# Rows for the last product in the spectrum's buffer, and a new table of times

## The chip, the cores and the metric

One core of a Trainium2 chip runs the whole program. The metric is the device time of one execution in microseconds (us). The engines are PE (TensorE: matmuls, with PEld for its weight loads), DVE (VectorE), ACT (ScalarE) and POOL (GpSimd); SP (SyncE) issues the transfers of the steady state. Each engine works through its own queue in order and waits there for what the next instruction needs.

## The reference

Input are 64 images of 96 x 56 x 56 in fp32. Each goes through two blocks:

```python
# block 0: convolution
out = silu(bn(expand_w @ x))                      # 1x1, 96 -> 192
out = channel_shuffle(shift_groups(out), 4)
out = silu(bn(bn(depthwise3x3(out)) + bn(id_w * out)))
se  = sigmoid(grouped1x1(relu(grouped1x1(mean(out)))))
x   = silu(bn(proj_w @ (out * se)) + x)           # 192 -> 96
# block 1: tokens t = 56*56 x 96
h = relu(bn(layernorm(t) @ w1.T))                 # 96 -> 192
X = fft(h, axis=tokens, norm='ortho')
X = relu(X.real*rd - X.imag*id + rb) + 1j*relu(X.imag*rd + X.real*id + ib)
t = t + bn(ifft(X).real @ w2.T)                   # 192 -> 96
t = t + ffn(layernorm(t))                         # 96 -> 384 -> 96, rounded to an 8-bit format
```

## The kernel before

The images go through some 60 kinds of step, each a small function `step(b, i)` for image `b` and part `i`. The transform over 3136 tokens is done in two stages of length 56: `f1` along one axis, `f2` along the other with the twiddles in its table, and `w2`, `i1`, `i2` back. Between the stages the data changes its layout by a trip through DRAM: `f1_st` writes the spectrum (`spec`), `f2_ld` reads it in four parts; `i1_st` writes `rows`, `i2_ld` reads them in two halves. A later part of each load is preceded by a tiny transfer into `probe` that reads what the earlier part brought, so SP waits there until that has landed.

The order of the work is written out by hand. `PLAN` gives each step and part a key, and the program is emitted in the order of `b * 105 + key`; every engine gets its instructions in that order. Keys of one image run from about -50 to over 370, so parts of up to four or five images are under way at a time. A key of 178.8 stands where the next image has 73.8. The numbers themselves set no time, only the order.

The steps, in the order in which an image meets them:

- `x_in` (SP) loads the image into `xi`, one buffer for all images. `ea_mm`/`ea_ev` and `eb_mm`/`eb_ev` (PE, ACT) expand, `eb_sh` (SP) shifts part of the channels from `e_u` into `e_b`, `eb_z` (POOL) clears its edge columns.
- `dw_mm`/`dw_ev` (PE, ACT), `gt`/`gs` and `lt`/`ls` (DVE, ACT) are three shares of the 3x3 convolution; `gt` and `lt` are nine passes of DVE each (L495, L508), `ls` is L511.
- `se1`, `se2` the gates; `se2_pw` (DVE) the gated weights; `pj_mm` (PE), `pj_add` (DVE, residual), `pj_ev` (ACT, L599) the projection into `t_buf`, of which there are three.
- `c_mm` (PE, L629), `c_st` (DVE, L637), `c_v`, `c_pow` (POOL, L656), `sp_v` (DVE, L661), `sp_mm` (PE), `sp_ev` (ACT), `sp_st` (SP) the statistics for the first norm.
- `w1_mm` (PE, L687) and `w1_ev` (DVE, L692) fill `h_v`; `f1_mm` (PE, L707), `f1_ev` (ACT, L719), `f1_st` (SP).
- `f2_ld` (SP) fills `g_v`; `f2_mm` (PE, L755 and L765), `f2_u` (ACT, L780), `f2_s` (DVE, L796 and L799), `f2_r` (ACT, L803), `f2_p` (DVE, L809) fill `pq_a` and `pq_b`.
- `w2_mm` (PE, L820 and L832), `w2_ev` (ACT, L850) fill `u_v`; `i1_mm` (PE, L859), `i1_ev` (ACT, L871) fill `q_v`; `i1_st` (SP).
- `i2_ld` (SP, L883 and L884) fills `p_v`; `i2_mm` (PE, L894), `i2_ev` (DVE, L906) add to `t_buf`.
- `n_mm` (PE, L607), `n_sq`, `n_v`, `n_pow` (POOL), `n_x`, `x_mm` (PE, L936), `x_ev` the second norm, turned by channels into `xq`; `h_mm` (PE, L949), `h_ev` (ACT, L954), `h_b` (DVE, L959), `h_q` (ACT, L965) and `o_mm` (PE, L971), `o_ev`, `o_b` (ACT, L981), `o_f` (POOL, L987), `o_st` (SP, L993) the last two products.

Two large buffers in SBUF serve several of these one after the other. `buf_h` holds `h_v`, then `pq_a` and `pq_b`, then `p_v`; `buf_g` holds `g_v`, then `u_v` (its first 2784 columns) and `q_v` (behind them). In PSUM, `psa` has two halves that `w1`, `f1`, `f2`, `w2`, `i1` and `i2` take in turn, and `psb` has four buffers for all other products.

PE's order of one period between the second product of the spectrum and the convolution, by the keys of before (a prime for each image further back): `f2_mm2'`, `se1_mm`, `f2_mm1'`, `h_mm7''`, `h_mm10''`, `se2_mm`, `o_mm1''`, `f2_mm3'`, `pj_mm0`, `pj_mm1`, `f2_mm4'`, `o_mm2''`, `w2_mm1'`, `h_mm9''`, `f2_mm5'`, `w2_mm0'`, `pj_mm2`, `pj_mm3`, `w2_mm2'`, `i1_mm0'`, two `h_mm''`, `i1_mm1'`, `h_mm18''`, `w2_mm3'`, two `h_mm''`, `c_mm2`, `c_mm0`, `i1_mm2'`, the other `c_mm`, four `eb_mm` of the next image, `sp_mm0`, three `ea_mm`, `i2_mm1'`, `i2_mm0'`, two `h_mm''`, `w1_mm0`, `sp_mm1`, `n_mm2'`, `n_mm0'`, `i2_mm3'`, `i2_mm2'`, `w1_mm1`, and so on to `f1_mm6`, `dw_mm`, `f2_mm0`, five small `h_mm` and `o_mm`.

Of the kernel before, what the change touches and what calls it, by code (L numbers as in the profile page):

```python
# [15 lines left out]
C = 96  # L16
# [19 lines left out]
NJ = HW // 2  # L36
# [7 lines left out]

PERIOD = 105.0000000
PLAN = {
    "x_in": (-47.0873800, -43.2480721, -33.8184146, -42.4321669, -41.6983245, -49.6354125, -45.2970245),
    "ea_mm": (25.6687554, -18.6019459, -18.2766274, 16.8947317, 9.0890490, -20.9491366, 26.5234594),
    "ea_ev": (26.5961203, -12.8346944, -12.0558905, 18.3539585, 11.9892739, -18.0927155, 26.8208273),
    "eb_mm": (-24.2217280, -27.1252465, -28.5212136, -26.0439145),  # L50
    "eb_ev": (-24.1705572, -24.8159248, -27.0548028, -24.4210050),
    "eb_sh": (-7.7763780, -5.1891020, -14.3493101, -8.0736385),
    "eb_z": (-0.0568513,),
    "dw_mm": (27.1905859, 28.2270849, 30.0157383),
    "dw_ev": (32.6265507, 32.5419044, 34.0136867, 32.0626837),
    "gt": (
        18.5417590, 27.3932657, 28.4348554, 30.0405776, 30.3534777, 31.2679969, 32.1252342, 33.5617949, 35.3971287,
    ),
    "gs": (37.3295953,),
    "lt": (-3.4369246, 1.4154043, 8.9015990, 12.7386339, 14.9242937, 16.9569681, 19.0058087, 25.8181102, 27.2536815),  # L60
    "ls": (30.9696760,),
    "se1_mm": (38.1174920,),
    "se1_ev": (39.4012005,),
    "se2_mm": (39.9568261,),
    "se2_ev": (41.0093676,),
    "se2_th": (41.6370568,),
    "se2_pw": (42.7356286,),
    "pj_mm": (47.6293895, 48.0460084, 55.6924205, 56.2257124),
    "pj_add": (51.9548047, 52.9757229, 48.9486048, 52.4199992, 56.5208084, 56.3342891, 57.7357223, 58.9053497),
    "pj_ev": (52.4266468, 54.5563910, 49.5686264, 53.9975302, 57.3353294, 58.0358601, 64.2278724, 60.1034130),  # L70
    "c_mm": (68.6422640, 72.8958869, 66.4186663, 70.5016788, 73.7968378, 81.1540053, 75.3642593),
    "c_st": (69.1048996, 74.0834508, 69.6641726, 71.8469708, 79.6401411, 81.2770733, 76.3014887),
    "c_v": (77.3368996, 84.7421070),
    "c_pow": (80.4785931, 85.6468413),
    "sp_v": (83.0231830, 86.9442643),
    "sp_mm": (83.5958606, 91.6622997),
    "sp_ev": (84.6935666, 98.3470105),
    "sp_st": (84.9182307, 104.3262665),
    "w1_mm": (91.1847046, 99.3743923, 107.0630638, 109.7535225, 115.0779331, 117.7791802, 128.3897698),
    "w1_ev": (95.1158413, 101.3844416, 109.5428488, 112.4130173, 118.6707781, 121.0948441, 130.1859056),  # L80
    "f1_mm": (103.1645366, 103.6378920, 112.1950558, 112.9967147, 121.9973686, 123.2339179, 131.7418102),
    "f1_ev": (103.8752244, 106.2876092, 115.0341529, 116.5416927, 123.1240239, 126.3577447, 132.9203119),
    "f1_st": (105.0265754, 116.1773780, 117.6886644, 118.9203869, 126.8918215, 126.9985321, 135.1083565),
    "f2_ld": (135.1419010, 135.4933209, 140.1563600, 153.2148099),
    "f2_mm": (135.3144599, 144.2623043, 142.7071223, 149.0540458, 153.9987769, 158.4518856),
    "f2_u": (
        137.6614180, 139.5999755, 145.8963285, 148.6480681, 143.6745056, 144.3798314, 151.9081888, 154.2916813,
        154.8766840, 155.4088772, 160.1561499, 160.2407000,
    ),
    "f2_s": (  # L90
        140.6001249, 141.6781807, 148.1048425, 149.2120807, 145.7714192, 145.9139389, 152.5732992, 154.5515294,
        156.3172941, 156.6391862, 160.5955754, 160.7678822,
    ),
    "f2_r": (143.2110272, 151.0363931, 149.4970293, 156.5551535, 160.8170295, 165.3808270),
    "f2_p": (145.3432078, 151.4176571, 149.5496523, 158.2621001, 161.1258051, 167.6494558),
    "w2_mm": (159.7753575, 155.3022495, 161.7965796, 168.1185810),
    "w2_ev": (161.2536676, 157.1569605, 163.6822311, 171.1138835),
    "i1_mm": (162.6590790, 166.7961018, 174.2991711),
    "i1_ev": (166.3472470, 165.9292538, 169.1177355, 169.1485805, 176.9253459, 176.6408078),
    "i1_st": (174.9466660, 180.3925690, 182.4974982),  # L100
    "i2_ld": (188.6796396, 198.8294222),
    "i2_mm": (192.8792346, 192.2221249, 201.7637940, 200.8210782),
    "i2_ev": (197.2438881, 196.4091824, 193.4196408, 195.1684356, 205.0085736, 204.5692890, 201.3823970, 201.8192486),
    "n_mm": (199.2735303, 219.3462979, 198.1616011, 209.7155720, 217.1048197, 206.4557874, 216.1525940),
    "n_sq": (200.3838494, 223.0303187, 198.7625009, 212.4039709, 219.3987946, 208.1995030, 218.5954397),
    "n_v": (200.8599777, 223.0993290, 200.2251649, 217.3989652, 220.1840919, 209.9338724, 219.1855594),
    "n_pow": (201.5854245, 224.4817921, 203.3394463, 218.3771210, 221.4663650, 210.8600116, 220.4581247),
    "n_x": (204.8989415, 227.0802149, 207.1755708, 219.2080326, 226.6324331, 212.4013872, 223.1334093),
    "x_mm": (205.9313777, 228.0541936, 214.7407205, 222.1417630, 227.6089704, 214.9482177, 224.9828165),
    "x_ev": (215.5949267, 230.5744237, 217.0784037, 224.8320339, 228.9853364, 216.6319969, 227.3901209),  # L110
    "h_mm": (
        232.6842970, 233.0509672, 234.5689910, 233.8905234, 243.9705701, 231.1824963, 242.0876641, 249.3422780,
        247.6714562, 262.3158746, 249.5121590, 269.1269742, 245.6772976, 281.8579222, 275.5176718, 291.0115353,
        298.8948961, 298.6901683, 272.9130353, 274.8890827, 267.7027131,
    ),
    "h_ev": (
        233.2951821, 233.9892274, 235.1790311, 235.3740739, 245.7427623, 232.8851785, 246.7755713, 250.3102318,
        248.5727503, 264.8834302, 250.8738180, 272.1122460, 247.3449184, 285.4922975, 280.0758001, 292.5182940,
        298.9075518, 299.1057623, 275.2554216, 280.8510059, 271.9477751,
    ),  # L120
    "h_b": (
        233.3310183, 238.5879932, 239.6985884, 236.4106010, 248.1860080, 237.7565907, 247.4859421, 252.4799898,
        253.3286109, 265.1753247, 274.5160827, 273.6196081, 259.8167793, 289.1079857, 281.7059923, 295.2166748,
        313.0427147, 307.8153028, 280.3205727, 295.0172563, 303.2860349,
    ),
    "h_q": (
        235.1365714, 240.0903826, 240.2123523, 238.6786534, 249.8236945, 239.5739109, 249.1205248, 258.5058367,
        256.0111952, 266.4473323, 276.4671451, 279.2778238, 261.0771312, 290.1247931, 282.3662819, 298.7249474,
        314.1209334, 326.2464381, 296.9278791, 328.6751318, 314.9292593,
    ),  # L130
    "o_mm": (243.3019756, 251.4566128, 260.0349491, 292.9513206, 292.0855692, 335.3427890, 334.7225136),
    "o_ev": (252.4449030, 252.4462979, 260.7877533, 295.5347424, 297.3701267, 339.4824442, 335.9297802),
    "o_b": (253.4669270, 274.1077430, 267.6272919, 297.7581544, 311.6604822, 343.9355403, 344.9555045),
    "o_f": (256.7737436, 286.0913549, 285.2670749, 323.3039842, 337.3903643, 352.8603345, 353.4120892),
    "o_st": (258.9714075, 288.2940604, 307.3848207, 328.4555594, 347.7179313, 355.7939648, 378.3559833),
}


# [1 line left out]
def conv_attn_ffn(  # L140
# [218 lines left out]
    buf_h = const.tile([128, C * HW + 8], F32, name="buf_h")  # L359
# [1 line left out]
    h_v = buf_h[:, 0 : NJ * MID].rearrange("p (b c) -> p b c", c=MID)  # L361
    pq_a = buf_h[:, 0 : NK * CP].rearrange("p (k f) -> p k f", f=CP)
    pq_b = buf_h[:, NK * CP : (NK + NS) * CP].rearrange("p (k f) -> p k f", f=CP)
    p_v = buf_h[:, 0 : NJ * C].rearrange("p (b o) -> p b o", o=C)

    buf_g = const.tile([128, (NK + 32) * C], F32, name="buf_g")
    nc.gpsimd.memset(buf_g, 0.0)
    g_v = buf_g[:, 0 : NK * MID].rearrange("p (k c) -> p k c", c=MID)
    u_v = buf_g[0:CP, 0 : NK * C]
    q_v = buf_g[0:CP, NK * C :]  # L370
    probe = const.tile([1, 8], F32, name="probe")


# [809 lines left out]
```

## Time and profile before

| | us |
|---|---|
| median of 3 runs | 6605.18 (6599.12 to 6605.9) |
| the profiled execution, whole | 6600.45 |
| its span, first to last instruction | 6598.6 |
| mean granted PE clock | 0.973 |
| `ls` (L511) runs first / last at | 74.8 / 6377.1 |

The span is cut by the profile into 40 slices; each digit is the busy share of a slice in tenths:

```profile
PE   4999999999999999999999999999999999999986
PEld 2666666666666666666666666666666666666664
DVE  6788787787887887887877878878878878778773
ACT  2677777777777777777777777777777777777776
POOL 1122222222222222222222222222222222222222
```

Between filling and draining all slices look alike: the 64 images pass at one steady pace, and one period of that pace shows the whole. A group in the profile is named by its line, its engine and what it writes from what; a wait is put down to the engine whose signal came last.

### The profile page before, as it was taken

How to read it: one execution, taken by the hardware profiler on the slowest of the kernel's cores; microseconds unless marked ns; L12 is line 12 of the kernel's file. 1: busy time of each engine (PE TensorE's matmuls, PEld its weight loads, DVE VectorE, ACT ScalarE, POOL GpSimd, SP SyncE). 2: the span in 40 equal slices, each digit the busy share in tenths (PEclk: the TensorE clock that was granted, in tenths of full speed). 3: DMA queues.
4: the chain of work that ended last, by engine and by line, in shares of the span. 5: the costliest groups of instructions: out<-in, count | busy, mean ns of one | idle time of the engine just before them, and what ended most of it. 6: DMA issues, size and time to landing. Idle time of an engine off the chain costs nothing.

```text
span 6598.6 us, 217772 instructions
## 1 busy us (share of the span) xinstructions
PE 5970.6 (90%) x92162; PEld 4023.3 (61%) x92162; DVE 5271.5 (80%) x9939; ACT 4990.7 (76%) x10830; POOL 1660.2 (25%) x1100
## 2 busy tenths in 40 slices
PE   4999999999999999999999999999999999999986
PEld 2666666666666666666666666666666666666664
DVE  6788787787887887887877878878878878778773
ACT  2677777777777777777777777777777777777776
POOL 1122222222222222222222222222222222222222
PEclk8999999999999999999999999999999999999997
DMA  3444444444444444444444444444444444444442
GB/s 83 105 113 119 112 110 120 117 107 118 114 116 116 116 114 115 112 116 113 110 121 117 107 118 114 116 116 111 118 111 109 123 112 111 120 118 106 121 103 74
DMA packets 976826, 740.73 MB, mean 112 GB/s; under 512 B 641745, under 2 KB 916889, under 8 KB 975721
## 3 DMA queue, kind: packets, MB, share of 16 engines
q1 hardware_dynamic: 973130, 725.03, 44.4%
q8 instruction: 725, 11.88, 0.8%
q10 hardware_dynamic: 2720, 1.77, 0.1%
q14 instruction: 251, 2.06, 0.1%
HBM read 329.68 MB, written 341.31 MB: 102 GB/s over the span
## 4 chain that ended last, share of the span: by engine, by line
DVE 30%; DMA 21%; ACT 21%; PE 13%; SPq 6%; issue 6%; POOL 3%; DVEq 0%; POOLq 0%; ACTq 0%
DMA buf_g<-spec 10%; DVE d_last L508 7%; DMA buf_h<-rows 6%; DVE ue L799 4%; DVE s L796 4%; ACT y L954 4%; ACT ue L780 3%; PE ps_eb L421 3%; DMA spec<-fs 3%; POOL rs L922 3%; PE psa L755 3%; ACT h L965 2%; DVE buf_h L809 2%; SPq L198 2%; DVE buf_h L692 2%
## 5 line engine op out<-in xcount | busy, mean ns | idle before, releaser
L987 POOL TENSOR_TENSOR o<-t,o 112x448 f32<-112x448 f32 x448 | 684.2, 1528 | 3322.6 <-ACT o L981 2100.4
L508 DVE SCALAR_TENSOR_TENSOR d_last<-e_b,taps,d_last 128x1568 f32<-128x1568 f32 x512 | 954.3, 1864 | 0.5
L965 ACT CAST h<-y 128x448 fp8e5<-128x448 f16 x1344 | 756.2, 582 | 236.8 <-DVE y L959 224.5
L922 POOL TENSOR_TENSOR rs<-v,mhalf 128x4 f32<-128x4 f32 x448 | 609.8, 1374 | 926.4 <-DVE v L623 669.9
L954 ACT CAST y<-ps_h 128x448 f16<-128x448 f32 x1344 | 679.4, 556 | 161.2 <-PE ps_h L949 158.1
L495 DVE SCALAR_TENSOR_TENSOR d_vec<-e_a,taps,d_vec 128x1120 f32<-128x1120 f32 x512 | 770.8, 1505 | 11.6
L687 PE MATMUL psa<-w1c,t 112*128 112x192 f32 x3584 | 684.9, 334 | 9.9 <-DVE t L906 9.7
L755 PE MATMUL psa<-l_tab,buf_g 128*64 128x112 f32 x7424 | 477.1, 287 | 233.0 <-DMA buf_g<-spec 191.6
L755 PEld LDWEIGHTS psa<-l_tab,buf_g 128*64 128x64 f32 x7424 | 419.9, 153 | 409.4 <-issue 271.8
L474 PE MATMUL ps_d<-e_a,diag 32*32 32x504 f32 x18432 | 629.4, 590 | 0.0
L929 ACT ACTIVATE xt<-ps_n,rs 128x96 fp8e5<-128x96 f32 x1792 | 465.4, 377 | 198.6 <-POOL rs L922 190.1
L687 PEld LDWEIGHTS psa<-w1c,t 112*128 112x128 f32 x3584 | 579.8, 190 | 50.8 <-DVE t L906 17.5
L959 DVE TENSOR_SCALAR y<-y,qb 128x448 f16<-128x448 f16 x1344 | 472.1, 371 | 112.7 <-ACT y L954 103.5
L809 DVE SCALAR_TENSOR_TENSOR buf_h<-ue,s 128x448 f32<-128x448 f32 (+2 forms) x768 | 423.7, 600 | 159.6 <-ACT s L803 157.9
L637 DVE BATCH_NORM_STATS2 st<-ps_c 128x6 f32<-128x96 f32 x1792 | 326.2, 251 | 278.7 <-PE ps_c L629 272.4
L474 PEld LDWEIGHTS ps_d<-e_a,diag 32*32 32x32 f32 x18432 | 395.7, 103 | 214.9 <-ACT e_a L411 37.9
L780 ACT ACTIVATE ue<-psa,fa 128x448 f32<-128x448 f32 (+1 forms) x512 | 346.5, 690 | 229.6 <-PE psa L755 124.7
L692 DVE SCALAR_TENSOR_TENSOR buf_h<-psa,rs 128x768 f32<-128x768 f32 x448 | 426.8, 953 | 69.6 <-PE psa L687 69.6
L656 POOL TENSOR_TENSOR rs<-v,mhalf 128x16 f32<-128x16 f32 (+1 forms) x128 | 333.6, 2606 | 582.8 <-DVE v L651 582.8
L949 PE MATMUL ps_h<-xq,q 96*128 96x448 fp8e5 x1344 | 409.1, 360 | 72.3 <-ACT y L954 45.3
L796 DVE SCALAR_TENSOR_TENSOR s<-psa,fa,ue 128x448 f32<-128x448 f32 (+1 forms) x512 | 325.5, 636 | 181.3 <-ACT ue L780 180.8
L906 DVE SCALAR_TENSOR_TENSOR t<-psa,bn2c_b,t 112x392 f32<-112x392 f32 x512 | 291.7, 621 | 155.2 <-PE psa L894 151.9
(172 smaller groups left out, 11948.6 us busy)
## 6 DMA issues: line engine op xcount, KB each, us to landing
spec<-fs SPq DMA_DIRECT2D x896, 192.0 KB
buf_g<-spec SPq DMA_DIRECT2D x384, 336.0 KB
buf_h<-rows SPq DMA_DIRECT2D x128, 672.0 KB
x<-in_x SPq DMA_DIRECT2D x896, 84.0 KB
out_dram<-o SPq DMA_DIRECT2D x896, 84.0 KB
rows<-buf_g SPq DMA_DIRECT2D x128, 420.0 KB
rows<-buf_g SPq DMA_DIRECT2D x64, 504.0 KB
e_b<-e_u SPq DMA_DIRECT2D x256, 105.1 KB
```

The lines of the kernel that those rows point to most:

```text
L474: nc.tensor.matmul(pss[r][j * 32 : j * 32 + 32], lhsT=diag[pr, tap, :], rhs=e_a[pr, r0 : r0 + SR, dx : dx + HW], start=tap == 0, stop=tap ...
L495: nc.vector.scalar_tensor_tensor(d_vec, win, w, d_vec, ALU.mult, ALU.add)
L508: nc.vector.scalar_tensor_tensor(d_last, win, w, d_last, ALU.mult, ALU.add)
L687: nc.tensor.matmul(ps[:, k, 0:MID], lhsT=t[:, n0 : n0 + 2 * TP], rhs=w1c, start=True, stop=True)
L692: nc.vector.scalar_tensor_tensor(h_v[:, js, :], held.pop(("w1", b, g))[:, :, 0:MID], 0.0, held["v", b][1][:, js].unsqueeze(2).to_broadcast ...
L755: nc.tensor.matmul(ps[c0 : c0 + 64, k, 0:CP], lhsT=g_v[:, k1, c0 : c0 + 64], rhs=l_tab[:, k1, :], start=True, stop=True,)
L796: nc.vector.scalar_tensor_tensor(held["s", b, i][:, q, 0:n, :], im, par[:, m : m + 1], a, ALU.mult, ALU.add)
L809: nc.vector.scalar_tensor_tensor(pq[:, k0 : k0 + n, q * HW : q * HW + HW], ue[:, q, 0:n, :], 0.0, s[:, q, 0:n, :], ALU.max, op)
L922: nc.gpsimd.tensor_tensor(rs, held.pop(("nv", b, g)), mhalf[:, 0:4], ALU.pow)
L954: nc.scalar.copy(y16, held.pop(("h", b, i)))
L965: nc.scalar.copy(held["h8", b, j][:, m, :], held.pop(("y", b, i)), saturate=False)
L987: nc.gpsimd.tensor_tensor(o32, rows, o16, ALU.add)
```

## The change

The view `p_v`, into which `i2_ld` loads the rows for the last product, moves from the front of `buf_h` to the front of `buf_g`: there it lies over `u_v`, and no longer over `h_v` and `pq_a`. All keys of `PLAN` are replaced; the steps, their instructions and the 105 between images stay.

```diff
-    "w1_mm": (91.1847046, 99.3743923, 107.0630638, 109.7535225, 115.0779331, 117.7791802, 128.3897698),
+    "w1_mm": (95.1879500, 93.7441300, 108.9329300, 114.8588500, 116.7257000, 125.5482100, 133.0065800),
...
-    "f2_ld": (135.1419010, 135.4933209, 140.1563600, 153.2148099),
+    "f2_ld": (152.6032700, 152.6042700, 163.1374800, 168.3891100),
...
-    "w2_mm": (159.7753575, 155.3022495, 161.7965796, 168.1185810),
+    "w2_mm": (169.3214300, 170.3892100, 177.6045500, 178.7672500),
...
-    "i1_mm": (162.6590790, 166.7961018, 174.2991711),
+    "i1_mm": (172.6133800, 179.2134300, 180.8411200),
...
-    "i2_mm": (192.8792346, 192.2221249, 201.7637940, 200.8210782),
+    "i2_mm": (196.2218200, 195.6861300, 201.0358200, 210.4878600),
...
     pq_a = buf_h[:, 0 : NK * CP].rearrange("p (k f) -> p k f", f=CP)
     pq_b = buf_h[:, NK * CP : (NK + NS) * CP].rearrange("p (k f) -> p k f", f=CP)
-    p_v = buf_h[:, 0 : NJ * C].rearrange("p (b o) -> p b o", o=C)
 
     buf_g = const.tile([128, (NK + 32) * C], F32, name="buf_g")
     nc.gpsimd.memset(buf_g, 0.0)
     g_v = buf_g[:, 0 : NK * MID].rearrange("p (k c) -> p k c", c=MID)
     u_v = buf_g[0:CP, 0 : NK * C]
     q_v = buf_g[0:CP, NK * C :]
+    p_v = buf_g[:, 0 : NJ * C].rearrange("p (b o) -> p b o", o=C)
```

PE's order by the new keys over the same stretch: `f2_mm2'`, `se1_mm`, `f2_mm1'`, `h_mm10''`, `h_mm18''`, `se2_mm`, `o_mm1''`, `f2_mm3'`, `pj_mm0`, `pj_mm1`, `f2_mm4'`, `w2_mm0'`, `o_mm2''`, `w2_mm1'`, `f2_mm5'`, `i1_mm0'`, `pj_mm2`, `pj_mm3`, `w2_mm2'`, `w2_mm3'`, `i1_mm1'`, `c_mm2`, `h_mm9''`, `c_mm0`, `h_mm14''`, `i1_mm2'`, `c_mm4`, `c_mm3`, `c_mm1`, `h_mm15''`, `eb_mm0`, `eb_mm3`, `c_mm6`, two `h_mm''`, `eb_mm1`, `eb_mm2`, three `ea_mm`, `c_mm5`, `sp_mm0`, `ea_mm1`, `h_mm19''`, `o_mm4''`, three `h_mm''`, `i2_mm1'`, `i2_mm0'`, `sp_mm1`, `w1_mm1`, `n_mm2'`, `n_mm0'`, `w1_mm0`, `i2_mm2'`, `f1_mm0`, `x_mm2'`, `o_mm3''`, `f1_mm1`, `i2_mm3'`, and so on to `f1_mm6`, `dw_mm`, `f2_mm0`, six small `h_mm` and `o_mm`.

On the other engines, as far as the prediction speaks of it: DVE has `f2_p0`, `se2_pw`, `h_b7`, `f2_s2`, `f2_p2`, `f2_s3`, `f2_s6`, `f2_p1`, `f2_s7` (before: `f2_p0` ahead of `f2_s4`, and `f2_s2`, `f2_s3`, `f2_p2`, `f2_p1`, `f2_s6`), later `f2_p4`, `f2_p5` and then the last four `pj_add` (before: these adds ahead of `f2_p5`), then `c_st0`, `c_st2`, `c_st4`, `c_st3`, `c_st1`, `c_v0`, `h_b14`, `sp_v0`, `h_b13`, `c_st6`, `h_b15`, `h_b20`, `c_st5`, `c_v1` (before: all `c_st` ahead of `sp_v0`). ACT has `i1_ev0`, `h_q18`, `i1_ev1`, `f2_r5`, `pj_ev5`, `pj_ev4`, `pj_ev6`, `w2_ev2` in this order, and `h_ev0`, `h_ev2` ahead of `f1_ev6`. POOL has `o_f1` ahead of `c_pow0`. SP has `i2_ld0`, `eb_sh0`, `sp_st0`, `eb_sh2`, `i2_ld1`, `o_st2`, `eb_sh1`, `eb_sh3` (before: `i2_ld0`, `sp_st0`, `eb_sh2`, `i2_ld1`, `eb_sh3`, `eb_sh0`, `o_st2`, `eb_sh1`), and `o_st3` ahead of `f2_ld0`.

## The prediction

> **What bounds the kernel now.** I read the page's engine totals first, then the waits of PE over one period, then the order of PE's work around its longest waits, and last the busy time by stretches. The silu of `d_last` (L511) runs first at 74.8 us and last at 6377.1, 63 periods of 100.04 us; 75 us of filling lie before it and 221 us of draining behind. So 1 us per period is worth 63 us, and a period is what has to be worked out.
>
> The engine totals:
>
> ```profile
> PE 5970.6 (90%) x92162; PEld 4023.3 (61%) x92162; DVE 5271.5 (80%) x9939; ACT 4990.7 (76%) x10830; POOL 1660.2 (25%) x1100
> ```
>
> The busy times of one period, and of stretches of it (columns: stretch and its length, then busy us of PE, PEld, DVE, ACT, POOL, then clock, DMA share, GB/s):
>
> ```profile
> 3000.00:3100.00 100.00, 92.79 (x1441) 62.62 (x1440) 81.67 (x154) 78.00 (x170) 25.63 (x18) 0.98 0.47 115
> 3063.22:3069.60 6.38, 3.51 (x39) 2.27 (x40) 6.24 (x7) 5.94 (x15) 0.00 (x0) 1.00 0.56 136
> 3069.60:3072.60 3.00, 3.00 (x35) 2.72 (x36) 2.96 (x6) 1.83 (x5) 1.30 (x1) 0.56 0.44 96
> 3005.00:3026.00 21.00, 19.61 (x318) 13.29 (x318) 12.70 (x56) 13.97 (x34) 6.73 (x5) 1.00 0.72 175
> 3026.00:3073.00 47.00, 42.82 (x668) 29.00 (x662) 44.70 (x53) 37.74 (x89) 15.01 (x11) 0.97 0.41 105
> ```
>
> PE works 92.8 of 100 us. DVE idles 8 of 21 us before 3026 and hardly at all in the 47 us after, while ACT is busy three quarters throughout: no single engine bounds, PE is nearest. What can be won or lost is its 7 us of idle, and these are its waits in that period:
>
> ```profile
> PE psa L755 <- DMA buf_g<-spec: 2.1, 2, 1.8
> PE psa L894 <- DMA buf_h<-rows: 1.2, 1, 1.2
> PE ps_o L971 <- ACT t L599: 1.0, 1, 1.0
> PE ps_h L949 <- ACT y L954: 0.7, 1, 0.7
> PE ps_n L607 <- ACT xq L943: 0.4, 1, 0.4
> PE ps_h L949 <- ACT d L483: 0.4, 1, 0.4
> PE psa L755 <- DVE ue L799: 0.4, 1, 0.4
> PE ps_x L936 <- ACT xt L929: 0.3, 1, 0.3
> ```
>
> In PE's order of work (start, us, then idle before it and its releaser):
>
> ```profile
> 3017.24 2.52 PE L894 MATMUL psa<-r_tab,buf_h 64*48 64x56 f32 x112
> ...
> 3024.35 2.52 PE L894 MATMUL psa<-r_tab,buf_h 64*48 64x56 f32 x112 [1.23 <-DMA buf_h<-rows]
> ...
> 3063.22 1.75 PE L755 MATMUL psa<-l_tab,buf_g 128*64 128x112 f32 x32 [0.37 <-DMA buf_g<-spec]
> ...
> 3069.60 2.93 PE L755 MATMUL psa<-l_tab,buf_g 128*64 128x112 f32 x32 [1.76 <-DMA buf_g<-spec]
> ...
> 3086.84 0.73 PE L971 MATMUL ps_o<-h,q 128*112 128x448 fp8e5 x3 [0.95 <-ACT t L599]
> ```
>
> The reader sees two loads that come late (rows, spectrum) and a PSUM buffer that comes late (`o_mm2` until the first `pj_ev`).
>
> **The edit of the buffer costs nothing by itself.** Instructions, shapes and DMA sizes stay; `i2_ld` still waits for the rows' store. In `buf_h` it takes away one wait: a new image's `w1_ev1` no longer stands behind the old image's last `i2_mm`. In `buf_g` it adds one: the next `f2_ld` must come after the last `i2_mm`. By the keys these are 105.5 and 152.6, 47 apart, so that wait is never reached (if cover were gone it would add at most the 1.26 us of one `i2_mm`). The same holds for `w1_ev` behind `w2_mm3`, 20 apart. What counts is the order, so I go along PE's new queue and see what each wait has as cover.
>
> **A, second half of the rows.** Now PE does two `h_mm`, `w1_mm0`, `sp_mm1`, `n_mm2`, `n_mm0` between the `i2_mm` of the first half and those of the second, and idles 1.23. In the new order it does `sp_mm1`, `w1_mm1`, `n_mm2`, `n_mm0`, `w1_mm0`: two `h_mm` (0.55) less, a `w1_mm` (1.47) more, 0.9 of cover. On SP the first `eb_sh` pair moves between the two `i2_ld`, with its two issues of 0.6; SP is then waiting for the first load (issued 3012.23, the probe runs at 3017.13), which hides them. Only one `i2_mm` follows at once; the other stands behind `f1_mm1`. Taken **-0.9**; ends -1.2 (wait gone) and 0 (the pair's bytes delay the loads as much).
>
> **B, `w2_mm0` in place of `o_mm2`.** The 0.95 of `o_mm2` goes: `w2_mm0` (2.3) now stands before it. But `w2_mm0` writes the `psa` half that `f2_s7` empties, and reads `f2_p1`, and DVE has both later. From the end of `f2_s5` (3077.04) DVE now does, spacing by the trace, `h_b`/`se2_ev` 0.43, `f2_p0` 1.11, `se2_pw` 0.78, then pairs of `f2_s` at 1.31 and `f2_p` at 1.11 as s2, p2, s3, s6, p1, s7: 0.43 + 1.11 + 0.78 + 4 x 1.31 + 2 x 1.11 = 9.8, until 3086.8. PE is through `f2_mm4` at 3085.85: a wait of 1.0. Net **+0.1**; ends -0.95 and +1.0 (`f2_u7` late too; `w2_mm1`, `f2_mm5`, `i1_mm0` are next in line).
>
> **C, `i1_mm1`.** After `pj_mm3` PE now does `w2_mm2` (2.3) and `w2_mm3` (1.6) and comes to `i1_mm1` 3.9 us later. That needs `w2_ev2`, on ACT behind `pj_ev5`, `pj_ev4`, `pj_ev6`, and those wait for DVE's `pj_add`s, queued behind `f2_p5`, which waits for `f2_r5`, which ACT has behind `i1_ev0`, `h_q18` and `i1_ev1`. With 0.58 (L871), 0.56 (L965), 0.68 (L803, 128x560) and 0.81 for `f2_p5` the last `f2_p` ends about 1.6 after `pj_mm3`; two adds 0.9, three `pj_ev` 1.6 and `w2_ev2` 0.8 make 4.9: a wait of 1.0. Now `w2_mm2`, `i1_mm0` and two `h_mm` lie there, `pj_ev4` to `pj_ev7` are spread around them, and nothing waits. If ACT runs 1 us ahead it is 0, if a further add is in the way 1.6; taken **+0.8**.
>
> **D, normalisation and expansion.** On DVE `sp_v0` now precedes `h_b13`, `c_st6`, `h_b15`, `h_b20`, `c_st5`, and it waits for `c_pow0` (2.93 on POOL, 3011.09), which has `o_f1` (1.30) ahead of it. `c_st6` holds one of four `psb` buffers meanwhile; PE has `h_mm20`, `h_mm13`, two `eb_mm` and three `ea_mm`, 4.6 us, for the other three before `c_mm5`. Taken **+0.5**; ends 0 and 2.9, the whole pow.
>
> **E, the spectrum.** PE still goes from `f1_mm6` through `dw_mm` (9.84) to `f2_mm0`. On ACT `f1_ev6` now follows `h_ev0` and `h_ev2` (0.45 each, half under `f1_mm6`): +0.5 on the store, the load and `f2_mm0`. `o_st3` now precedes `f2_ld0` on SP, in the 3.4 us in which SP waits for the store (3054.0 to 3057.42). Six small steps instead of five fill the wait before `f2_mm2`: -0.3. Net **+0.2**; ends -0.3 and +1.5.
>
> The waits of `w1_mm`, `x_mm` and `n_mm` (0.18, 0.26, 0.43) change place: `x_mm2` has 4.5 of cover instead of 10, against `n_sq` 0.45, `n_v` 0.65, pow 1.0 to 2.45, `n_x` 1.0 and hand-overs, 3.5 to 5. I leave their sum.
>
> Sum: -0.9 + 0.1 + 0.8 + 0.5 + 0.2 = **+0.7 per period**, 63 x 0.7 = 44. From `ls` to the last `o_f` the keys have 321.1 against 322.4 before, so filling and draining get 0, by these few us. The profiled execution took 6600.45 (span 6598.6), which is 0.07% under the median of 6605.18: 6600.45 + 44 = **6645**. All low ends give -2.45 a period, 6446; all high ends +7.0, 7041.
>
> **The clock.** The row: `f2_mm2` took 2.93 at a granted clock of 0.56 after the idle stretch, and the same 32 records took 1.75 at 1.00 in the period at 3170. If B's and C's waits of 1 us cost the same 1.2 us once per period, the sum would be 6600.45 + 63 x 1.9 = 6720. The Trainium skill ("TensorE: Matmul & The Clock Gate", Part 1) puts the drop after an idle window of about 3.4 us, by which waits of 1 us cost nothing and 6645 stands; the trace has it after waits of 0.42, 0.69 and 1.76 with work between, so it is less clear-cut than the page.
>
> **Rivals.** *The freed buffer pays (30%).* `w1_ev1` runs in DVE's idle stretch before 3026 and takes load from the full 47 us; A at -1.2, B at -0.95, C and D covered: -2.15 a period, **6465**. For it: DVE's 8 us of idle just there. Against it: in both orders `f2_mm2` waits for the load, not for DVE. *A block at `sp_v0` (14%).* D at 2.9 because `c_st6` and `c_st5` stand behind the pow, `psb` runs out, and `c_mm5`, `sp_mm1` and so `w1_mm` shift: 2.6 to 2.9 in place of 0.5 gives 2.8 to 3.1 a period, **6777 to 6796**; it decides once DVE's stop exceeds the 4.6 us of PE's cover. *It cancels (9%).* The load chain from `f1_mm6` to `f2_mm2` (16.5 us) is equal in both orders and the rest sums to zero: **6600**; then the freed buffer frees no time of PE, and the change is one of order alone. *Small gain (9%)*: A -0.9, B -0.5, C +0.8, D 0, E +0.2: -0.4, **6575**.
>
> **Numbers.** The sum, a small loss (6618 to 6720), has 38%. No change is within 0.2% (13 us), about what this measurement can tell. Faster 30 + 9 = 39%, within 9%, slower 38 + 14 = 52%. The range that leaves two in ten out reaches into both outer rivals: 6480 to 6810; the likeliest case alone 6618 to 6720.
>
> **What will show it.** A: the wait of L894 on rows below 0.4 us per period. B: the L971 wait on L599 gone, a wait of about 1 at L820 on DVE. C: about 1 at L859 on ACT's L850. D: DVE idle before L661 with POOL as releaser, PE waits at L629, L421 or L406. E: `f2_mm0` waiting about 0.9. The prediction is wrong if PE's idle sum stays under 6.5 us per period, or if waits appear at L707, L687 or L607.

## The result and the profile after

| | before | after |
|---|---|---|
| median, us | 6605.21 (4 runs) | 6681.10 (6677.43 to 6686.11, 4 runs) |
| the profiled execution / its span, us | 6600.45 / 6598.6 | 6678.35 / 6676.4 |
| mean granted PE clock | 0.973 | 0.965 |
| `ls` (L511) runs first / last at | 74.8 / 6377.1 | 75.7 / 6452.8 |
| one of the 63 periods, us | 100.04 | 101.22 |

The change makes the kernel slower: ratio 1.0117, 95% interval 1.010 to 1.0135. The forecast was 6645, with 6618 to 6720 for its likeliest case. Filling and draining are 1 and 2 us longer; the rest, 63 x 1.18 = 74 us, is in the period, as the sum had assumed.

The engine totals of the page after:

```profile
PE 6076.4 (91%) x92162; PEld 4054.1 (61%) x92162; DVE 5409.2 (81%) x9939; ACT 5047.1 (76%) x10830; POOL 1595.2 (24%) x1100
```

The instruction counts are those of before, yet PE is busy for 106 us longer and DVE for 138. The same work got slower, on two engines. PE's waits in one period of after (3180 to 3281 us; columns: us in total, times, longest):

```profile
PE psa L755 <- DMA buf_g<-spec: 2.4, 2, 1.7
PE psa L820 <- ACT ue L780: 2.1, 1, 2.1
PE ps_h L949 <- ACT y L954: 1.1, 1, 1.1
PE ps_c L629 <- DVE st L637: 0.3, 1, 0.3
PE psa L687 <- DVE t L906: 0.2, 1, 0.2
PE psa L859 <- ACT buf_g L850: 0.2, 1, 0.2
```

Of the list of before, the waits on the rows, on `t` (L599), on `xq`, on `xt` and on `d` are gone; one new wait of 2.1 us at L820, the first `w2` product, has nearly the size of the spectrum's. Its place in PE's order (start, us, then the idle before and its releaser):

```profile
3217.34 1.95 PE L585 MATMUL ps_pj<-d_last,pw 64*112 64x504 f32 x8
3219.22 1.56 PE L765 MATMUL psa<-l_tab,buf_g 128*64 128x112 f32 x28
3222.84 2.51 PE L820 MATMUL psa<-w2a,buf_h 128*64 128x96 f32 x32 [2.06 <-ACT ue L780]
3225.28 1.51 PE L832 MATMUL psa<-w2b,buf_h 64*64 64x96 f32 x32
3226.72 0.78 PE L971 MATMUL ps_o<-h,q 128*112 128x448 fp8e5 x3
3227.42 1.53 PE L820 MATMUL psa<-w2a,buf_h 128*64 128x96 f32 x32
3228.89 0.88 PE L832 MATMUL psa<-w2b,buf_h 64*64 64x96 f32 x32
...
3255.46 2.52 PE L894 MATMUL psa<-r_tab,buf_g 64*48 64x56 f32 x112
...
3262.86 1.33 PE L894 MATMUL psa<-r_tab,buf_g 64*48 64x56 f32 x51
```

After its wait `w2_mm0` takes 2.51 + 1.51 us; `w2_mm1`, the same 32 + 32 products 4.6 us later, takes 1.53 + 0.88. The busy times of that stretch and of the next one show why (stretch and length, busy us of PE, PEld, DVE, ACT, POOL, then clock, DMA share, GB/s):

```profile
3220.00:3227.00 7.00, 4.94 (x84) 4.26 (x79) 6.89 (x13) 2.28 (x5) 0.00 (x0) 0.76 0.01 2
3227.00:3235.00 8.00, 8.00 (x103) 5.58 (x103) 4.63 (x11) 7.21 (x13) 0.00 (x0) 1.00 0.42 88
```

A mean clock of 0.76 over 7 us is 3.4 us at half speed. And DVE is busy through the whole wait: PE waits for DVE's queue, though the releaser named is ACT's `f2_u`. What DVE did just before, and POOL beside it:

```profile
3211.59 1.15 DVE L809 SCALAR_TENSOR_TENSOR buf_h<-ue,s 128x448 f32<-128x448 f32 x2
...
3214.58 0.68 DVE L799 SCALAR_TENSOR_TENSOR ue<-psa,fb,ue 128x448 f32<-128x448 f32 x1
3215.18 2.26 DVE L809 SCALAR_TENSOR_TENSOR buf_h<-ue,s 128x448 f32<-128x448 f32 x2
3217.36 0.67 DVE L796 SCALAR_TENSOR_TENSOR s<-psa,fb,ue 128x448 f32<-128x448 f32 x1
...
3215.35 1.60 POOL L987 TENSOR_TENSOR o<-t,o 112x448 f32<-112x448 f32 x1 [16.59 <-ACT o L981]
```

The two instructions of `f2_p0` take 1.15 us; the same two of `f2_p2` take 2.26, and just then POOL's `o_f0` runs. In the order of before `o_f0` was over when `f2_p2` began, and `f2_p2` and `f2_p1`, four instructions, took 2.22 together:

```profile
3078.99 1.30 POOL L987 TENSOR_TENSOR o<-t,o 112x448 f32<-112x448 f32 x1 [7.58 <-ACT o L981]
3081.76 2.22 DVE L809 SCALAR_TENSOR_TENSOR buf_h<-ue,s 128x448 f32<-128x448 f32 x4
```

It is so throughout: after, `o_f0` falls on `f2_p2` in each of periods 12 to 54, and `f2_p2` takes 2.25 to 2.26 us; before, it does so in none, and `f2_p2` takes 1.15.

Averages over periods 12 to 54, added up from the trace's instructions, make the account of a period: PE's idle went from 7.71 to 7.27 us, the clock's loss (time at half speed, halved) from 1.86 to 2.83, and the remainder, 0.65, passed inside instructions counted as busy. -0.44 + 0.97 + 0.65 = 1.18, the whole loss. Of the 0.65, 0.38 lie in the first convolution products (`dw_mm0`, from 3.52 to 3.90); no run separates what made these longer. With a few periods more or less the clock's loss moves by up to 0.07.

### The profile page after: what moved, and what is told of

Read it like the earlier page. It is cut to its first block, busy times and chain, and to the rows that moved or that the text cites. A ratio compares the mean times of both kernels' runs of the same rounds, so it can differ in the third digit from the quotient of the medians.

```text
span 6676.4 us, 218591 instructions
## 1 busy us (share of the span) xinstructions
PE 6076.4 (91%) x92162; PEld 4054.1 (61%) x92162; DVE 5409.2 (81%) x9939; ACT 5047.1 (76%) x10830; POOL 1595.2 (24%) x1100
## 4 chain that ended last, share of the span: by engine, by line
DVE 35%; PE 31%; ACT 11%; DMA 10%; issue 6%; POOL 5%; SPq 3%; ACTq 0%; POOLq 0%; DVEq 0%
PE psa L687 8%; DVE d_last L508 7%; DVE d_vec L495 6%; DMA buf_g<-spec 5%; PE ps_n L607 5%; POOL rs L656 5%; DVE buf_h L809 4%; PE psa L707 4%; DVE s L796 4%; DVE ue L799 4%; PE psa L859 3%; ACT ue L780 3%; PE psa L894 3%; DVE ps_pj L593 2%; DVE st L637 2%
## 5 line engine op out<-in xcount | busy, mean ns | idle before, releaser
L987 POOL TENSOR_TENSOR o<-t,o 112x448 f32<-112x448 f32 x448 | 705.2, 1580 | 4143.2 <-ACT o L981 4083.4
L508 DVE SCALAR_TENSOR_TENSOR d_last<-e_b,taps,d_last 128x1568 f32<-128x1568 f32 x512 | 989.3, 1932 | 9.7 <-POOL e_b L447 0.6
L495 DVE SCALAR_TENSOR_TENSOR d_vec<-e_a,taps,d_vec 128x1120 f32<-128x1120 f32 x512 | 820.3, 1602 | 11.5
L954 ACT CAST y<-ps_h 128x448 f16<-128x448 f32 x1344 | 686.5, 540 | 68.8 <-PE ps_h L949 60.8
L687 PE MATMUL psa<-w1c,t 112*128 112x192 f32 x3584 | 680.0, 336 | 14.3 <-DVE t L906 13.9
L755 PEld LDWEIGHTS psa<-l_tab,buf_g 128*64 128x64 f32 x7424 | 420.5, 153 | 387.1 <-issue 305.7
L474 PE MATMUL ps_d<-e_a,diag 32*32 32x504 f32 x18432 | 654.1, 590 | 0.8 <-ACT e_a L411 0.8
L755 PE MATMUL psa<-l_tab,buf_g 128*64 128x112 f32 x7424 | 478.0, 287 | 192.8 <-DMA buf_g<-spec 180.2
L922 POOL TENSOR_TENSOR rs<-v,mhalf 128x4 f32<-128x4 f32 x448 | 518.9, 1166 | 442.8 <-DVE v L623 435.3
L687 PEld LDWEIGHTS psa<-w1c,t 112*128 112x128 f32 x3584 | 575.4, 191 | 73.9 <-issue 38.9
L809 DVE SCALAR_TENSOR_TENSOR buf_h<-ue,s 128x448 f32<-128x448 f32 (+2 forms) x768 | 482.8, 670 | 88.2 <-ACT s L803 88.2
L474 PEld LDWEIGHTS ps_d<-e_a,diag 32*32 32x32 f32 x18432 | 409.4, 103 | 226.6 <-ACT e_a L411 37.1
L820 PE MATMUL psa<-w2a,buf_h 128*64 128x96 f32 (+1 forms) x7424 | 388.8, 260 | 130.2 <-ACT ue L780 123.8
L692 DVE SCALAR_TENSOR_TENSOR buf_h<-psa,rs 128x768 f32<-128x768 f32 x448 | 428.1, 956 | 59.4 <-PE psa L687 54.4
L949 PE MATMUL ps_h<-xq,q 96*128 96x448 fp8e5 x1344 | 400.4, 361 | 80.5 <-ACT y L954 69.5
L959 DVE TENSOR_SCALAR y<-y,qb 128x448 f16<-128x448 f16 x1344 | 427.7, 330 | 50.2 <-ACT y L954 49.4
L820 PEld LDWEIGHTS psa<-w2a,buf_h 128*64 128x64 f32 (+1 forms) x7424 | 337.6, 137 | 198.7 <-ACT ue L780 134.9
```

Source lines behind the costliest of these rows:

```text
L474: nc.tensor.matmul(pss[r][j * 32 : j * 32 + 32], lhsT=diag[pr, tap, :], rhs=e_a[pr, r0 : r0 + SR, dx : dx + HW], start=tap == 0, stop=tap ...
L495: nc.vector.scalar_tensor_tensor(d_vec, win, w, d_vec, ALU.mult, ALU.add)
L508: nc.vector.scalar_tensor_tensor(d_last, win, w, d_last, ALU.mult, ALU.add)
L687: nc.tensor.matmul(ps[:, k, 0:MID], lhsT=t[:, n0 : n0 + 2 * TP], rhs=w1c, start=True, stop=True)
L755: nc.tensor.matmul(ps[c0 : c0 + 64, k, 0:CP], lhsT=g_v[:, k1, c0 : c0 + 64], rhs=l_tab[:, k1, :], start=True, stop=True,)
L809: nc.vector.scalar_tensor_tensor(pq[:, k0 : k0 + n, q * HW : q * HW + HW], ue[:, q, 0:n, :], 0.0, s[:, q, 0:n, :], ALU.max, op)
```

## The experiments

Each run was timed beside the kernel before on the same chip (6610.7 to 6616.6 there). "The wait" is PE's mean per period, over the same periods as above.

**1. `o_f0` off `f2_p2`.** The changed kernel; only `o_b0`, for which `o_f0` waits, is later.

```diff
-    "o_b": (272.0951800, 289.6102500, ...
+    "o_b": (274.4300000, 289.6102500, ...
```

> The changed kernel with one key changed: o_b0 (ACT) goes behind f2_u9, so that POOL's o_f0 no longer runs beside f2_p2 on DVE. Theory (o_f0 on POOL doubles f2_p2, that makes the 2.0 us wait of w2_mm0, and the wait drops the clock): f2_p2 back from 2.26 to 1.15 us, the wait of w2_mm0 to about 1.0, the second clock drop of each period (1.0 us lost) gone or nearly: 1.0 to 2.0 us per period of 63, 6555 to 6620 us. Rival (w2_mm0 waits for f2_u8 and f2_u9 on ACT, the releaser that the profile names): wait and clock as they are, 6665 us or more.

Measured: 6573.61 us, ratio to before 0.9944 (0.9928 to 0.9960): 108 us less than the changed kernel (114, if each is taken against the kernel before on its own chip), and faster than the kernel before. The wait of `w2_mm0` is 0.90 instead of 2.04, and the clock's loss 1.93 instead of 2.83. One line of each profile says the same, the groups of L809 by form (busy us, mean ns of one, over the execution); before, after, and this run:

```profile
L809 DVE SCALAR_TENSOR_TENSOR buf_h<-ue,s 128x448 f32<-128x448 f32 x512 | 305.6, 648 | 2.0 <-ACT s L803 0.3
```

```profile
L809 DVE SCALAR_TENSOR_TENSOR buf_h<-ue,s 128x448 f32<-128x448 f32 x512 | 364.7, 754 | 45.0 <-ACT s L803 45.0
```

```profile
L809 DVE SCALAR_TENSOR_TENSOR buf_h<-ue,s 128x448 f32<-128x448 f32 x512 | 295.1, 619 | 3.6 <-ACT s L803 3.6
```

The place in PE's order, in this run:

```profile
3183.79 1.53 PE L820 MATMUL psa<-w2a,buf_h 128*64 128x96 f32 x32 [0.96 <-DVE ue L799]
```

The mean goes 648, 754, 619 ns, and behind a wait of 0.96 the 32 products take 1.53 us again, the full clock. ACT's `o_b0` itself, which the edit moves as well, is not what held PE up: in the changed kernel ACT stands idle for 1.51 us soon behind it, until DVE's L809 is done, and in this run the releaser named at L820 is DVE. So one POOL instruction in the wrong place, not the order of the products, costs about 108 us.

**2. The same collision made in the kernel before.** `o_b0` is shifted there so that `o_f0` falls on `f2_p2`.

```diff
-    "o_b": (253.4669270, 274.1077430, ...
+    "o_b": (254.6000000, 274.1077430, ...
```

> The kernel before with one key changed: o_b0 (ACT) behind f2_r2, so that POOL's o_f0 falls on f2_p2 and f2_p1 of DVE. Theory (POOL's o_f stretches DVE's instructions that read and write SBUF alone, and that stretch reaches PE): f2_p over 2 us for the pair that is hit, the wait of o_mm2 longer by about 1.1 us, perhaps a clock drop of 1.0 behind it: 1.1 to 2.1 us per period, 6675 to 6740 us. Rival (the stretch is hidden): 6605 within 15.

Measured: 6719.9 us, ratio 1.0165 (1.014 to 1.019). The group of L809 in this run:

```profile
L809 DVE SCALAR_TENSOR_TENSOR buf_h<-ue,s 128x448 f32<-128x448 f32 x512 | 370.9, 775 | 1.9 <-ACT s L803 0.5
```

The wait of `o_mm2`, which stands at this place in the order of before, went from 0.81 to 1.89 us, and the clock's loss from 1.86 to 3.52. ACT is idle for 1.30 us soon behind the later `o_b0` here too, so it is again not the limit. The collision is enough by itself, in either order, so the cause is shown from both sides.

**3. The buffer alone.** The kernel before, `p_v` at three other places, each a run of its own.

```diff
-    p_v = buf_h[:, 0 : NJ * C].rearrange("p (b o) -> p b o", o=C)
+    p_v = buf_g[:, 0 : NJ * C].rearrange("p (b o) -> p b o", o=C)
```

> The kernel before with only the view p_v moved to buf_g; its table of times stays. Theory (the order alone decides; the buffer's two waits are never reached): 6605 us within 13, and the wait of the second i2_mm on its rows stays at 1.2 us per period. Rival (the buffer itself moves time, by another wait on buf_g or by taking one off buf_h): more than 20 us either way.

```diff
+    p_v = buf_h[:, NJ * C : 2 * NJ * C].rearrange("p (b o) -> p b o", o=C)
```

> The kernel before, with p_v in the second stretch of buf_h's columns (NJ*C to 2*NJ*C) instead of the first; nothing else changed. p_v in buf_g cost 36 us in the kernel before, with a second half of the load that took 6.83 us instead of 6.33. Theory (it is the buffer: where the rows land in buf_g, their load meets other traffic of the same buffer or another wait): 6600 to 6615, the load at 6.3 us. Rival (any place other than the first columns of buf_h does it, since another hazard is tracked): 6640 to 6655, the load at 6.8 us.

```diff
+    p_v = buf_g[:, NK * C : (NK + NJ) * C].rearrange("p (b o) -> p b o", o=C)
```

> The kernel before with p_v behind the first 2784 columns of buf_g, over q_v, instead of at buf_h's front; nothing else changed. In the first columns of buf_g it cost 36 us (6646.9), in the second stretch of buf_h nothing (6608.3). Theory (landing in buf_g at all makes the second half's load longer, 6.9 instead of 6.4 us from issue to the product): 6635 to 6655. Rival (only the first columns of buf_g do it): 6600 to 6615, the load at 6.4 us.

| rows land in | us | ratio (95%) | second half, from issue to the product | wait on it | clock's loss |
|---|---|---|---|---|---|
| `buf_h`, first columns (before) | 6611 | 1 | 6.41 us | 1.21 | 1.86 |
| `buf_h`, second stretch | 6608.3 | 0.9995 (0.9985 to 1.0005) | 6.48 | 1.31 | 1.89 |
| `buf_g`, first columns | 6646.88 | 1.0054 (1.0035 to 1.0073) | 6.89 | 1.73 | 2.21 |
| `buf_g`, behind them | 6652.83 | 1.0062 (1.0049 to 1.0076) | 6.94 | 1.82 | 2.28 |

In `buf_g`, at both places, the second half of the rows comes 0.4 to 0.5 us later, though it is issued at the same distance from the first half's product (0.68 to 0.76 us behind its start); the first half isn't slower (5.05 against 5.07 us). The packets in the traces say the same: the last one of the second half ends 5.54 and 5.62 us behind the issue in `buf_h`, 5.96 and 6.04 in `buf_g`, and the packets of 6724 bytes of the shift (`eb_sh`) beside it last 540 and 535 ns against 572 and 585. Why they are slower stays open. Nor is it so in every order: with SP's order of after, where other transfers follow the second half, its last packet ends 5.08 us behind the issue in `buf_g` (the second run of experiment 5). The wait grows by 0.5 to 0.6 us and the clock's loss by 0.35 to 0.4. One such wait, in the run with `p_v` at the front of `buf_g`:

```profile
3034.66 2.52 PE L894 MATMUL psa<-r_tab,buf_g 64*48 64x56 f32 x112
3042.41 4.05 PE L894 MATMUL psa<-r_tab,buf_g 64*48 64x56 f32 x112 [1.86 <-DMA buf_g<-rows]
```

The same 112 products take 2.52 us in the first half and, behind a wait of 1.86, 4.05. The second stretch of `buf_h` is free of the same hazard (`w1_ev1` writes columns 768 to 1535, `p_v` lies from 2688 on), and it brings nothing. So an earlier free buffer is worth nothing by itself, and this buffer costs some 40 us in this order, where the rows' load is not covered.

**4. A alone.** The kernel before with `p_v` in `buf_g` and `w1_mm1` put between `n_mm0` and `i2_mm3`, so ahead of the second half (the second expectation names the place loosely); then the same with `p_v` in the second stretch of `buf_h`.

```diff
-    "w1_mm": (91.1847046, 99.3743923, ...
-    "w1_ev": (95.1158413, 101.3844416, ...
+    "w1_mm": (91.1847046, 94.9000000, ...
+    "w1_ev": (95.1158413, 96.2000000, ...
```

> The kernel before with p_v in buf_g and two keys changed, w1_mm1 and w1_ev1 ahead of the second pair of i2_mm (the part of the new order that the buffer allows). Theory (A: 1.5 us more of PE work covers the rows' load): the wait of 1.2 us on the rows gone, 63 x 1.2 = 75 us, 6530 us. Rival (the time comes back at the next wait, because DVE or the spectrum's load sets the end of the stretch): 6595 to 6615 us, with the wait before f2_mm0 or f2_mm2 longer by as much.

> The kernel before with w1_mm1 in front of n_mm2 (as in the run that gave 6582.0) and p_v in the second stretch of buf_h's columns instead of buf_g. Theory (order A and the buffer add up: -65 for the order, +36 for buf_g): 6540 to 6560. Rival (with w1_mm1 in front the second half of the load is covered in both buffers): 6575 to 6590. If the freed first columns of buf_h are what matters rather than buf_g, it is also 6575 to 6590.

Measured: 6581.96 us, ratio 0.9956 (0.9940 to 0.9972), 65 us under the same buffer without the move; and in `buf_h` 6569.68, ratio 0.9931 (0.9917 to 0.9946). The wait on the rows falls to 0.35 and 0.13 us; a new one of 1.13 appears at L607, where `n_mm5`, which `w1_mm1` kept apart from the last `i2_mm`, now waits for its additions (L906). Both times lie between the ranges of theory and rival: the old wait goes, and the new one takes part of the gain back. A pays, and more than its own new wait costs. Whether `buf_h` is better than `buf_g` here (12 us, intervals that overlap) isn't settled.

**5. A undone in the changed kernel.** First `w1_mm0` alone goes behind `i2_mm2`; then `w1_ev0` moves along with it.

```diff
-    "w1_mm": (95.1879500, 93.7441300, ...
+    "w1_mm": (96.5000000, 93.7441300, ...
```

> The changed kernel with w1_mm0 put back behind i2_mm2, so that between the first half of the last product and i2_mm2 PE has a 128-wide product less to do (about 1.5 us). Theory A (the w1 product in front is what hides the second half of the rows' load, 1.19 -> 0.11 us of wait per period): the wait of L894 on rows comes back by 1.0 to 1.5 us per period, 63 to 95 us, and the time is 6740 to 6775. Rival (other work hides the load now, such as the changed order on SP): the rows' wait stays under 0.4 us and the time at 6675 to 6690.

```diff
-    "w1_ev": (98.2073200, 93.7451300, ...
+    "w1_ev": (99.6000000, 93.7451300, ...
```

> The changed kernel with w1_mm0 behind i2_mm2 on PE and, unlike the run before, w1_ev0 behind i2_mm2's two additions on DVE too, so that no product waits for an addition that stands behind w1_ev0. Theory A (the w1 product in front hides the second half of the rows' load): the wait on rows comes back by 0.8 to 1.5 us per period, the wait of L707 on L906 (2.12 us in the run before) is gone, and with a further clock dip of 0 to 1 us the time is 6730 to 6830. Rival (the loss of the run before was the additions' queue and not the load): 6680 to 6700.

Measured: 6964.95 us, ratio 1.0527 (1.0499 to 1.0556), a miss of 190 us; and 6812.45, ratio 1.0291 (1.0262 to 1.0320), inside its range, though not by the waits that were expected. In the first run `f1_mm0` waits 2.12 us for an addition (L906) that DVE has behind `w1_ev0`, which itself waits for the late `w1_mm0`; the clock's loss is 4.64. In the second, one period reads:

```profile
3026.53 1.43 PE L894 MATMUL psa<-r_tab,buf_g 64*48 64x56 f32 x56 [0.30 <-DMA buf_g<-rows]
3027.89 1.57 PE L687 MATMUL psa<-w1c,t 112*128 112x192 f32 x8
3030.51 0.88 PE L707 MATMUL psa<-buf_h,f_tab 56*64 56x384 f32 x8 [1.05 <-DVE buf_h L692]
```

The mean wait on the rows is 0.69 instead of 0.12 (0.85 in the first run), so it came back by 0.57, less than the 0.8 to 1.5 of the theory. The rest of the loss is the 1.05 of `f1_mm0`, which comes straight behind the product whose eviction it reads, and 0.34 of clock: 0.57 + 1.05 + 0.34 = 1.96 of the 2.08 us per period. So the `w1` product is the load's cover, but the price of taking it away is mostly another wait; A's own size is better read from experiment 4.

**6. Both causes taken out.** Experiment 1 with `p_v` in the second stretch of `buf_h`.

> The changed kernel with o_b0 later (as in the run that gave 6573.6) and p_v in the second stretch of buf_h's columns instead of buf_g. Theory (the edit of the buffer costs a few tenths of a us per period wherever the rows' load is near the path): 6540 to 6570, clock loss per period 1.7 to 1.9. Rival (in the new order the second half of the rows has cover, so its half us costs nothing): 6565 to 6580, the same as with buf_g.

Measured: 6569.55 us, ratio 0.9931 (0.9916 to 0.9946). The time fits theory and rival alike; the waits fit the rival. It is 4 us from experiment 1, no difference that the runs can tell: in the new order the second half has its cover (6.68 and 6.69 us from issue to the product, waits of 0.00 and 0.09), and the buffer costs nothing here. This kernel and the last of experiment 4 are the fastest of the study.

**7. What is left of B.** In experiment 6's kernel `h_b7` leaves DVE's queue ahead of `f2_s2`.

```diff
     "h_b": (
-        250.7318300, ..., 269.0530200,
+        250.7318300, ..., 274.1500000,
...
     "h_q": (
-        254.5419900, ..., 273.6090500,
+        254.5419900, ..., 274.4250000,
```

> The version with o_b0 later and p_v in buf_h's second stretch (6569.6), with h_b7 (0.25 us from start to start on DVE) moved from ahead of f2_s2 to behind f2_s7, and h_q7 moved along with it. Theory (in B's place DVE's queue is without a gap, so each instruction less ahead of f2_s7 is a shorter wait of w2_mm0): the wait at L820 goes from 0.94 to about 0.7 us per period and the time to 6550 to 6560. Rival (ACT's f2_u6 and f2_r2 set the pace as much, or o_mm2 is late instead): 6565 to 6580.

Measured: 6581.86 us, ratio 0.9939 (0.9921 to 0.9957), no gain, and just above the rival's range. The wait of `w2_mm0` fell by 0.11 us and those of `w2_mm1` and `o_mm2` grew by 0.06 each. So the 0.25 us taken out of DVE's queue did not come through, and the theory that this queue alone sets the wait fell. That the clock's loss is 2.20 here against 1.85 in experiment 6, around `f2_mm2`, is left unexplained.

**8. E undone.** Experiment 6 with `f1_mm6` and `f1_ev6` ahead of `h_mm0`, `h_mm2`, `h_ev0` and `h_ev2`.

```diff
-    "f1_mm": (..., 131.1398300, 142.0593800),
-    "f1_ev": (..., 134.4331000, 142.9930700),
+    "f1_mm": (..., 131.1398300, 140.5000000),
+    "f1_ev": (..., 134.4331000, 141.9000000),
```

> The version with o_b0 later and p_v in buf_h's second stretch (6569.6), with E undone: f1_mm6 ahead of h_mm0 and h_mm2 on PE and f1_ev6 ahead of h_ev0 and h_ev2 on ACT. Theory E (the two evictions ahead of f1_ev6 put the spectrum's load back by 0.8 us, and half of that or more shows as wait of f2_mm0): the load lands 0.8 us earlier against the convolution's end, f2_mm0's wait falls from about 1.0 to 0.2 to 0.6, the time to 6520 to 6550. Rival (the convolution then waits for the buffers that h_ev0 and h_ev2 empty, and gives it back): 6560 to 6590, with dw_mm longer than 10.24 us per period.

Measured: 6604.36 us, ratio 0.9977 (0.9966 to 0.9988): the direction of the rival, and beyond its range. The groups of L755 and L474 in experiment 6 (busy us, mean ns, then the idle before and what ended it), and then in this run:

```profile
L474 PE MATMUL ps_d<-e_a,diag 32*32 32x504 f32 x18432 | 654.6, 590 | 0.8 <-ACT e_a L411 0.8
...
L755 PE MATMUL psa<-l_tab,buf_g 128*64 128x112 f32 x7424 | 481.6, 289 | 188.8 <-DMA buf_g<-spec 174.9 <-DVE ue L799 12.5 <-DVE gate L547 0.9
```

```profile
L474 PE MATMUL ps_d<-e_a,diag 32*32 32x504 f32 x18432 | 711.5, 590 | 21.2 <-issue 10.3 <-ACT e_a L411 1.8
...
L755 PE MATMUL psa<-l_tab,buf_g 128*64 128x112 f32 x7424 | 467.0, 283 | 62.6 <-DMA buf_g<-spec 48.4 <-DVE ue L799 12.6 <-issue 0.6
```

The spectrum's load, PE's largest wait, falls from 174.9 to 48.4 us, and the kernel gets 35 us slower: the convolution's busy and idle time grows by 57 + 20 us, as the rival had it: `h_ev0` and `h_ev2`, which empty buffers that the convolution writes, come later now, and the waits for L954 (`h_ev`) ahead of L474 and its weight loads go from 18.9 to 79.5 us. Besides, the wait per period at `f2_mm1` (L765) grows from 0.33 to 0.96, and 0.5 is new at `se1_mm` (L518).

## Why the prediction was right, and where it was not

Direction, place and size of the result fell into the likeliest case: a small loss, from waits that change place between the same work. That the direction came out was luck in part: without B's collision, which the sum did not contain, the same order in the same buffer gains 0.6 us per period (experiment 1), where the sum had a loss of 0.7. Of its terms, per period:

| step | predicted | measured |
|---|---|---|
| A, rows' second half | -0.9 | -1.09 (1.21 to 0.12) |
| B, `w2_mm0` in place of `o_mm2` | +0.1 | +1.2 of wait (0.81 to 2.04), and +1.0 of clock behind it |
| C, `i1_mm1` | +0.8 | +0.17 |
| D, `c_mm5` | +0.5 | +0.26 |
| E, spectrum | +0.2 | -0.1 (+0.22 at `f2_mm0`, -0.31 at `f2_mm2`) |
| other waits | sum left open | about -0.7 (`xq`, `xt`, `d` gone, `y` +0.43; the others cancel) |

The measured waits add up to -0.2; the other -0.2 of the -0.44 of idle time lies in gaps under 0.15 us, which the lists of waits leave out.

**A** was right in mechanism and size. The wait is gone from the period shown, and experiment 4 has the move alone at 65 us, 1.03 a period, with its new wait at L607 counted in.

**B is the term that was mis-sized.** "A wait of 1.0" for `w2_mm0` was right for DVE's queue as it was added up, 9.8 us from `f2_s5` to `f2_s7`: with `o_f0` out of the way the run measures 0.90. The working left out POOL, beside which `f2_p2` takes 1.1 us longer, and took +1.0 as the upper end of the net term ("`f2_u7` late too"). Measured are +1.2, and the clock behind it. Both parts vanish in experiment 1 and come in experiment 2. Of the 76 us, B's excess alone would be more than all; the smaller C, D, E and the gains left open paid part of it.

**C** was mis-sized the other way: the `pj_add` and `pj_ev` that should have taken 0.9 and 1.6 us take 0.73 and 1.3 from start to start, `w2_ev2` 0.67, and the last `f2_p` ends 1.24 us behind `pj_mm3` instead of 1.6: 3.94 in all, against the 3.9 of cover, where 4.9 had been added up from busy times. Back to back, an instruction here can start before the one ahead has ended in the records (above, L799 starts at 3214.58 and takes 0.68, and L809 starts at 3215.18), so busy times added up are too long.

**D** and **E** had the right places: the new 0.26 at L629, and `f2_mm0` at 1.03 instead of the forecast 0.9. `w1`, `f1` and `n` got no new wait (L687 0.15 to 0.20), and PE's idle of 7.27 stayed over the 6.5 named as the mark of a wrong prediction.

**"The edit of the buffer costs nothing by itself" was wrong** for the order it was argued in. The hazards were read rightly, none of them is reached; but in that order the load into `buf_g` takes 0.4 to 0.5 us more, which costs 36 to 42 us where it ends PE's wait; behind A's cover in the new order the runs show no cost. The prediction priced the waits of a place, not the transfer to it.

**The clock.** The paragraph gave 1.2 us per period if waits of 1 us dropped the clock, and none by the page. For waits of that length none was right: at 0.8 to 1.1 us the table at the end has no drop. But the wait became 2.04, and that costs 1.0 on average (27 drops in 45 periods, 1.7 us each). The Trainium skill ("TensorE: Matmul & The Clock Gate", Part 1) ties the drop to an idle window of about 3.4 us that runs freely. The trace agrees on the length: a low stretch lasts 3.41 us or a multiple. It does not agree that so long an idle time is needed: 2.04 us with work on both sides were enough in 27 of 45 periods.

**The rivals.** The freed buffer, at 6465, had a wrong premise: experiment 3 shows the freed place to be worth 0. The block at `sp_v0` didn't come (0.26 at L629 instead of 2.9). Yet the faster side was near: without `o_f0`'s collision the new table gives 6573.6, where the small gain had 6575, though by other terms.

## What to carry to other kernels

An order is not only what stands ahead of what on each queue: two instructions on different engines, with no data between them, can hold each other up, so look at what runs on POOL during the DVE work that PE waits for. A wait of PE is to be priced by its length, because the clock can drop behind it: in these orders a single wait of about one microsecond cost itself, and one of two cost half as much again. And the largest wait is not the largest gain: in experiment 8 it went from 2.5 to 0.5 us a period and the time went up.

## What the runs showed of the hardware

**POOL and some DVE instructions take turns.** `o_f` (L987), a sum of two SBUF operands on POOL, takes 1.30 us alone. A DVE instruction with two SBUF operands that begins while it runs ends only behind it. In the changed kernel the first instruction of `f2_p2` has begun 0.17 us ahead of `o_f0` and takes its usual 0.62, and `o_f0` takes 1.60; the second begins 0.36 us behind the start of `o_f0`, takes 1.73 and ends 0.49 behind it. So do other passes that begin beside L987: L495 takes 2.31 or 2.42 instead of 1.39, L508 2.57 instead of 1.85, and L647, on 16 columns, 0.95 instead of 0.17. Where a pass of L508 had begun 0.37 us earlier, in the kernel before, it kept its 1.84 and L987 took 2.63. Instructions that read PSUM stayed as they were: L799 684 ns in both cases, L692 957 and 954, L906 618 and 617. L959, a 16-bit operation on one SBUF operand, waits as well: 0.86 instead of 0.33 in the kernel before, begun 0.57 behind L987. Summed over a period, DVE lost 2.4 us to L987 before, 4.5 after and 3.4 in experiment 1. The 2.1 between the first two are nearly all of what DVE's busy time grew by, 138 us in 63 periods. The Trainium skill ("SBUF — State Buffer", Who interferes with whom) states which instructions contend: a DVE instruction with two SBUF inputs with a GpSimd instruction that reads SBUF, and one with at most one SBUF input outside the two-port modes not. The runs agree for the instructions with two SBUF operands and for those that read PSUM; whether L959 ran in such a mode, no trace here shows.

**The longer the wait of PE, the more often its clock drops.** Of 45 periods, so many had a drop of 3.41 us or more right behind the wait named:

| kernel | wait | mean us | periods with a drop |
|---|---|---|---|
| experiments 1, 6, 7 | `w2_mm0` | 0.8 to 0.9 | 0 |
| experiment 5, second run; experiment 4 | `f1_mm0`; `n_mm5` | 1.05; 1.13 | 0 |
| before; second stretch of `buf_h` | second half of the rows | 1.21; 1.31 | 4; 6 |
| `p_v` in `buf_g`, two places | second half of the rows | 1.73; 1.82 | 12; 14 |
| experiment 2 | `o_mm2` | 1.89 | 31 |
| after | `w2_mm0` | 2.04 | 27 |
| experiment 5, two runs | `w2_mm0` | 1.82; 2.00 | 13; 15 |
| experiment 5, first run | `f1_mm0` | 2.12 | 39 |

The share grows with the wait, and within one kernel too: before, the four waits with a drop lasted 1.90 us on average, the others 1.13. But waits of like length differ by a factor of two and more, so what lies around the wait counts too: in experiment 8 `f2_mm2`, close behind a wait of 1.17 at L949, has a drop in 12 of 45 periods, with a wait of 0.84 there on average. No run separates that.
